# Another order of pairs in a quad's last slot, and the first norm's result turned in blocks on VectorE and placed by way of DRAM

## The chip, the cores and the metric

The kernel runs on one core of a Trainium2 chip (trn2). Its engines are TensorE (PE in the profile), VectorE (DVE), ScalarE (ACT), GpSimd (POOL) and SyncE (SP, which here only issues DMAs). The metric is the device time of one execution, in microseconds, on that core.

## The reference

One decoder layer over 16 sequences of 512 tokens with 256 features, all in float32. Attention has 16 heads of 16 features, a LoRA term on q and v, rotary positions and a causal mask. The feed-forward part is a product up to 1024, ten butterfly stages, Gelu, ten butterfly stages and a product down to 256. A layer norm without weights follows each part.

```python
q = query @ wq + query @ Aq @ Bq * 4.0
k = query @ wk
v = query @ wv + query @ Av @ Bv * 4.0
q, k = rope(split_heads(q)), rope(split_heads(k))
attn = softmax(where(causal, -1e9, q @ k.T / sqrt(16)))
x = layernorm(x + merge_heads(attn @ v) @ wo)          # the first norm
h = butterfly(x @ W_exp + b_exp, up_weights)
h = gelu(h + up_bias)                                  # exact
y = butterfly(h, down_weights) @ W_con + b_con + down_bias
x = layernorm(x + y)                                   # the second norm
```

Both butterflies are linear, so the kernel folds them into the two weight matrices once (`fold_tasks`), and then runs two plain products for each sequence.

## The kernel before

**Batches, quads, slots.** A sequence is called a batch, b from 0 to 15. Its 16 heads are handled as four quads of four heads, (c, par) with c and par in 0 and 1. The four heads of a quad lie in four groups of 32 rows of TensorE, and heads 0 and 1 are its pair 0, heads 2 and 3 its pair 1. The 512 x 512 scores of a head are cut in four blocks of 128 rows or columns, of widths 512, 384, 256 and 128 because of the causal mask. A quad takes five slots (`PER_QUAD = 5`), so that a batch takes 20 (`per`). The main loop runs over slots, `for s in range(-head, last)`. In this text u is a slot's place in its quad (s mod 5), and n its place among the 20 of a batch (s mod 20).

**Two passes over the scores.** Each slot holds two pieces of work. `largest` (L420 on TensorE, L429 on VectorE) computes scores of the quad of this slot to find each row's largest value: VectorE reads the score tile with a reduction into `junk` and `mx`. `weights` (L477, L494, L498) computes scores of the quad of 15 slots earlier (`behind`), transposed and with the largest already subtracted by an extra row. ScalarE takes their Exp from the score tile into `pT`, and POOL's affine_select clears the masked part. One slot later `weigh` (L521) multiplies pT with the values into `po`; after a quad's last group, `normalize_heads` copies po on ScalarE (L540) and issues two or three DMAs on SP.

**Score tiles.** There are only two, of two PSUM banks each: `pb` (pair0 in the code) and `pa` (pair1). In slots with u from 0 to 3, `weights` writes pb, read by ScalarE, and `largest` writes pa, read by VectorE. The two work on different pairs of heads, so that their matmuls run side by side in different row groups. In slots with u = 4 both write half of each of the two tiles, pair 0 in pb and pair 1 in pa.

**Order.** The schedule is written by hand. Every engine works through its instructions in program order, and the program's order is: the matmuls of a slot, then what reads them, then `weigh` of earlier slots, then the list `others[s]` (filled by `add(s, f, ...)`), then the list `holes[s]`, then fold tasks. The matmuls outside the scores thus stand between the scores of one slot and the next, while ScalarE and VectorE empty pb and pa; they are called fillers below. With s = 20 b, the fillers and the other steps that matter stand at:

- `project_v` (L383, one matmul pair for each of four blocks t), four slots; its result is copied into `vaug` on ScalarE (L390)
- `start_projection` (L337, 16 matmuls of 128x512), for the next batch, four at s + 10, as holes; followed by `turn` (rotary, on POOL) and `part`
- `project_out` (L559) at s + 41 and s + 42; then the first norm: `spread` (VectorE, then a pow on POOL), `offset` (VectorE), `centre` (ScalarE, four instructions)
- `turn_x1` (L616, L617) at s + 45: eight transposes on TensorE with `ident`, two copies on VectorE into `x1T`, then one addition of biases on POOL (L621)
- `hidden` (L633): eight chunks hc, two a slot, from s + 46; copied to `h` by ScalarE or VectorE
- `gelus` (L651): eight instructions on ScalarE, at s + 50, with a table load before and after
- `contract` (L660): four blocks t in two halves, at s + 51, 52, 53, 55, 56, 58, 60, 63; after a second half VectorE adds (L668) and takes the statistics
- `spread`, `offset`, `centre`, `store` for the second norm at s + 63 to s + 68

So the later steps of batch b run two batches after its scores began, beside the scores of batches b + 1 and b + 2. The last two batches have an order of their own behind the last score slots (`edge`, `end`).

Of the kernel before, what the change touches and what calls it, by code (L numbers as in the profile page):

```python
# [11 lines left out]
F32 = mybir.dt.float32  # L12
# [5 lines left out]
P = 128  # L18
# [15 lines left out]
def decoder_layer(  # L34
# [345 lines left out]
    def project_v(b, t):  # L380
        pv = bank(f"pvv_{b}_{t}", [P, D])
        for d in range(NC):
            nc.tensor.matmul(  # L383
                pv,
                xTs[b][:, d, t * P : (t + 1) * P],
                wv_sb[:, d, :],
                start=(d == 0),
                stop=(d == NC - 1),
            )
        nc.scalar.copy(  # L390
            vaugs[b % 2][:, t, :, 1 : 1 + 2 * HG].rearrange("p g (h i e) -> p g h i e", h=2, e=2)[
                :, :, :, :, 0
            ],
            pv.rearrange("p (g h i) -> p g h i", h=2, i=DH),
        )
# [14 lines left out]
    def largest(b, c, par, placed):  # L410

        q, k_ = qz[b % NR][c], kz[b % NR][c]
        mms, later = [], []
        for block, pair, ps, at in placed:
            n, t = width(block), NT - 1 - block
            for i in range(2):
                g = 2 * pair + i
                rows = slice(HG * g, HG * g + (HG if par else DH))
                mms.append(
                    lambda i=i, rows=rows, at=at, n=n, t=t, ps=ps: nc.tensor.matmul(  # L420
                        ps[:, i, at : at + n],
                        q[rows, par, t * P : n],
                        k_[rows, par, 0:n],
                        start=True,
                        stop=True,
                    )
                )
                later.append(
                    lambda i=i, at=at, n=n, t=t, g=g, ps=ps: nc.vector.tensor_tensor_reduce(  # L429
                        out=junk[:, 0:n],  # L430
                        in0=ps[:, i, at : at + n],
                        in1=causal[:, T - n : T],
                        scale=-1.0,
                        scalar=HUGE,
                        op0=ALU.add,
                        op1=ALU.min,
                        accum_out=mxs[c][:, par, g, t : t + 1],
                    )
                )
        return mms, lambda: [f() for f in later]  # L440

    def place_largest(b, c):

# [16 lines left out]
    def weights(b, c, par, placed):  # L460

        qt, kt = qz[b % NR][c], kz[b % NR][c]
        group = placed[0][0]
        key = ("pT", b, c, par, group)
        if key not in state:
            state[key] = ppool.tile(
                [P, NG, T], F32, tag="pT", name=f"pT_{b}_{c}_{par}_{group}"
            )
        pT = state[key]
        mms = []  # L470
        for block, pair, ps, at in placed:
            n = width(block)
            for i in range(2):
                g = 2 * pair + i
                rows = slice(HG * g, HG * g + (HG if par else DH + 1))
                mms.append(
                    lambda i=i, rows=rows, at=at, n=n, k=block, ps=ps: nc.tensor.matmul(  # L477
                        ps[:, i, at : at + n],
                        kt[rows, par, k * P : (k + 1) * P],
                        qt[rows, par, k * P : T],  # L480
                        start=True,
                        stop=True,
                    )
                )

        def after():
            for pair in range(2):
                mine = [(block, ps, at) for block, r, ps, at in placed if r == pair]
                if not mine:
                    continue  # L490
                n = sum(width(block) for block, _, _ in mine)
                ps, at = mine[0][1:]
                heads = slice(2 * pair, 2 * pair + 2)
                nc.scalar.activation(pT[:, heads, 0:n], ps[:, :, at : at + n], AF.Exp)  # L494
                at = 0
                for block, _, _ in mine:
                    diag = pT[:, heads, at : at + P]
                    nc.gpsimd.affine_select(  # L498
                        out=diag,
                        in_=diag,  # L500
                        pattern=[[0, 2], [1, P]],
                        compare_op=ALU.is_ge,
                        fill=0.0,
                        base=0,
                        channel_multiplier=-1,
                    )
                    at += width(block)

        return mms, after

    def weigh(b, c, par, group):
        pT = state.pop(("pT", b, c, par, group))
# [95 lines left out]
            )  # L608


    def turn_x1(b, c):
        if c == 0:
            state["x1T", b] = ring2.tile([P, NC, T], F32, tag="x1T", name=f"x1T_{b}", bufs=1)
        pt = bank(f"pt1_{b}_{c}", [P, NT, P])
        for t in range(NT):
            nc.tensor.transpose(pt[:, t, :], zs[b][:, t, c * P : (c + 1) * P], ident)  # L616
        nc.vector.tensor_copy(  # L617
            state["x1T", b][:, c, :], pt.rearrange("p t q -> p (t q)")
        )
        if c == NC - 1:  # L620
            nc.gpsimd.tensor_tensor(  # L621
                zs[b],
                zs[b],
                bias2[:, 0:1, :].to_broadcast([P, NT, D]),
                ALU.add,
            )

    def hidden(b, hc, fused=False):
        if hc == 0:
# [2 lines left out]
        for c in range(NC):  # L632
            nc.tensor.matmul(  # L633
                ph,
                wup[:, c, hc * P : (hc + 1) * P],
                state["x1T", b][:, c, :],
                start=(c == 0),
                stop=(c == NC - 1),
            )
# [72 lines left out]
    for b in range(B):  # L712
        s = b * per
        if b > 0:

            at = {1: (-16, -11, -13, -9), B - 1: (-1, 10, 10, 14)}.get(b, (-3, -1, 4, 14))
            for t in range(NT):
                add(s + at[t], project_v, b, t)
        if b + 1 < B:

            add(s - head * (b == 0), load_xT, b + 1)
            at = {0: (2, 5, 7, 10), 1: (3, 6, 8, 11)}.get(b, (10, 10, 10, 10))
            for i, (c, side) in enumerate(chains):
                holes.setdefault(s + at[i], []).append(
                    lambda b=b, side=side, c=c: start_projection(b + 1, side, c)
# [2 lines left out]
                for step in range(3):  # L728
                    add(turning + step, turn, b + 1, side, c, step)
                for step in range(1 + side):  # L730
                    add(turning + (6 if i == 3 else 4) + step, part, b + 1, side, c, step)
        add(s + 9, load_x, b)
        add(s + 11, place_largest, b, 0)
        add(s + 21, place_largest, b, 1)
        for c in range(NC if b + 1 < B else 1):
            for t in range(NT):
                at = (27, 28, 29, 31) if c == 0 else (36, 37, 39, 40)
                add(s + (at[t] if b + 1 < B else 29 + t), normalize, b, c, t)
        if b + 1 < B:
            for t in range(NT):  # L740
# [1 line left out]
            add(s + 42, spread, 1, b)  # L742
            add(s + 43, offset, 1, b)
            add(s + 44, centre, 1, b)
            for c in range(NC):
                add(s + 45 + (b + 2 == B), turn_x1, b, c)
        if b + 2 < B:
            for hc in range(NHC):
                add(s + 46 + hc // 2, hidden, b, hc)
            holes.setdefault(s + 50, []).insert(0, lambda b=b: gelus(b))  # L750
            for t in range(NT):
                for half in range(2):
                    at = (11, 12, 13, 15, 16, 18, 20, 23)[2 * t + half]
                    if b + 3 == B and t == NT - 1:
                        at = (23, 25)[half]
                    add(s + 40 + at, contract, b, t, half)
            add(s + 63 + 2 * (b + 3 == B), spread, 2, b)
            add(s + 66, offset, 2, b)
            add(s + 68, centre, 2, b)
            add(s + 68, store, b)  # L760

# [41 lines left out]
    first, second = fold_tasks()  # L803
    fold = first + second
    tasks_at = dict(zip(range(2, behind), (0, 1, 2, 3, 4, 4, 5, 5, 5, 6, 9, 11, 14)))
    for s in range(behind, 2 * per + 5):
        tasks_at[s] = len(first) + -(-len(second) * (s - behind + 1) // (2 * per + 5 - behind))
    ahead = 0
    given = 0
    due = deque()  # L810
# [12 lines left out]
    for s in range(-head, last):  # L823
# [4 lines left out]
            if 0 <= n < B * per  # L828
        ]
        parts = []  # L830
        step = 2
        if kinds and not (len(kinds) == 1 and kinds[0][2] % 2):
            u = kinds[0][2]
            pair0 = ps_b.tile([P, 2, T], F32, tag="b", name=f"pb_{s}")
# [147 lines left out]
```

## Time and profile before

| | us |
|---|---|
| median of 3 runs | 1386.91 |
| range of the runs | 1386.61 to 1389.14 |
| profiled execution | 1387.34 |
| its span, first to last instruction | 1385.6 |
| TensorE busy | 1355.0 (98%) |
| VectorE busy | 916.0 (66%) |
| ScalarE busy | 713.1 (51%) |
| POOL busy | 509.5 (37%) |
| mean granted TensorE clock | 0.987 |

Reading the rows: an instruction row gives its start in the span and its duration in microseconds, the engine, the line, the operation, what it writes <- what it reads, and its shapes; square brackets at its end give the idle time of the engine before it and who ended that. Matmuls are pipelined and their ends modelled, so a row of TensorE ends some 0.07 us after the next can start. A float32 matmul is two instructions. Rows of the chain of waits give start, duration and the work that the end of the span hung on. A window row gives each engine's busy time in a stretch, then the granted clock and the DMA share.

### The profile page before, as it was taken

To read this page: it belongs to the slowest core of one execution; us is meant where nothing else is said; L and a number is where in the kernel's file an instruction comes from. 1 tells how busy PE (TensorE), PEld (TensorE's weight loads), DVE (VectorE), ACT (ScalarE), POOL (GpSimd) and SP (SyncE) were. 2 spreads that over 40 slices of the span, in tenths; PEclk is the share of its full clock that TensorE was granted. 3 is DMA by queue.
4 is the path that set the end of the run, shared out by engine and by line. 5 is a ranking of instruction groups with operands and counts; after the bars stand their busy time and mean duration, and the time that the engine had idled before them with its cause. 6 is when DMAs were issued, how large, how long until landed. Compare 5 with 4: busy or idle time off the path is not lost.

```text
span 1385.6 us, 23937 instructions
## 1 busy us (share of the span) xinstructions
PE 1355.0 (98%) x8760; PEld 719.7 (52%) x8760; DVE 916.0 (66%) x2937; ACT 713.1 (51%) x1101; POOL 509.5 (37%) x777
## 2 busy tenths in 40 slices
PE   8999999999999999999999999999999999998998
PEld 4445545455454545545454555545455554544455
DVE  5667757667585766758576675857677585765532
ACT  2576454554545455454545555454555545454543
POOL 3425215344352534435153433515343351531311
PEclk9899999999999999999999999999999999999999
DMA  5311010110201011020101102010110201010000
GB/s 169 117 40 48 25 55 29 42 42 29 74 29 66 29 43 41 29 74 29 66 29 43 40 29 72 31 66 29 43 40 29 74 29 67 14 43 9 29 12 31
DMA packets 45685, 63.49 MB, mean 46 GB/s; under 512 B 5752, under 2 KB 26232, under 8 KB 45568
## 3 DMA queue, kind: packets, MB, share of 16 engines
q1 hardware_dynamic: 41680, 56.42, 11.5%
q10 hardware_dynamic: 3888, 5.55, 1.3%
q8 instruction: 69, 1.13, 0.3%
q14 instruction: 48, 0.39, 0.1%
HBM read 23.40 MB, written 8.91 MB: 23 GB/s over the span
## 4 chain that ended last, share of the span: by engine, by line
PE 94%; DVE 3%; ACT 2%; issue 1%; DMA 0%; POOL 0%; POOLq 0%; DVEq 0%; ACTq 0%
PE pb L477 20%; PE py L660 17%; PE ph L633 17%; PE po L521 11%; PE pqk L337 8%; PE pa L420 5%; PE pvv L383 5%; PE pwo L559 4%; PE pd L267 2%; PE pb L420 1%; DVE junk L429 1%; PE pa L477 1%; PE pt L616 1%; ACT pT L494 1%; PE fold L219 1%
## 5 line engine op out<-in xcount | busy, mean ns | idle before, releaser
L429 DVE CUSTOM_DVE_ANT_0 junk<-pa,causal 128x384 bf16<-128x384 f32 (+2 forms) x878 | 438.5, 499 | 216.0 <-PE pa L420 182.8
L494 ACT ACTIVATE pT<-pb 128x1024 f32<-128x1024 f32 (+1 forms) x314 | 293.9, 936 | 372.1 <-PE pa L420 255.6
L498 POOL TENSOR_SCALAR_AFFINE_SELECT pT<-pT 128x256 f32<-128x256 f32 x512 | 201.9, 408 | 755.2 <-ACT pT L494 751.1
L477 PE MATMUL pb<-qz,kz 17*128 17x512 f32 (+2 forms) x1756 | 330.2, 475 | 11.6 <-ACT pT L494 9.9
L420 PE MATMUL pa<-kz,qz 32*128 32x384 f32 (+3 forms) x1756 | 323.8, 468 | 1.7 <-DVE mx L429 1.7
L660 PE MATMUL py<-wdn,h 128*128 128x256 f32 x1024 | 254.1, 392 | 1.4 <-ACT h L651 1.4
L633 PE MATMUL ph<-x1T,yb 128*128 128x512 f32 x512 | 237.6, 608 | 1.8 <-DVE x1T L617 1.8
L477 PEld LDWEIGHTS pb<-qz,kz 17*128 17x128 f32 (+1 forms) x1756 | 142.5, 184 | 173.5 <-issue 92.3
L660 PEld LDWEIGHTS py<-wdn,h 128*128 128x128 f32 x1024 | 185.8, 190 | 75.8 <-issue 37.0
L521 PE MATMUL po<-pT,vaug 128*32 128x512 f32 (+3 forms) x2048 | 180.1, 447 | 0.0
L420 PEld LDWEIGHTS pa<-kz,qz 32*128 32x128 f32 (+1 forms) x1756 | 149.3, 185 | 22.4 <-ACT vaug L390 9.6
L633 PEld LDWEIGHTS ph<-x1T,yb 128*128 128x128 f32 x512 | 92.9, 191 | 125.4 <-issue 98.6
L553 DVE RECIPROCAL sums<-sums 128x128 f32<-128x128 f32 x128 | 121.2, 947 | 0.0
L646 ACT COPY h<-ph 128x512 f32<-128x512 f32 x86 | 50.3, 585 | 134.8 <-PE ph L633 134.8
L337 PE MATMUL pqk<-xT,wqk 128*128 128x512 f32 x256 | 119.1, 616 | 0.0
L429 DVE CUSTOM_DVE_ANT_0 junk<-pb,causal 128x256 bf16<-128x256 f32 (+3 forms) x146 | 63.6, 435 | 73.5 <-ACT pT L494 66.1
L521 PEld LDWEIGHTS po<-pT,vaug 128*32 128x32 f32 x2048 | 47.1, 109 | 101.7 <-issue 88.9
L429 DVE DVE_READ_ACCUMULATOR2_ANT mx<- 128x1 f32 x1024 | 84.6, 83 | 0.0
L337 PEld LDWEIGHTS pqk<-xT,wqk 128*128 128x128 f32 x256 | 48.1, 194 | 61.1 <-issue 57.6
L602 ACT ACTIVATE z<-z,norm 128x256 f32<-128x256 f32 x128 | 66.8, 593 | 24.9 <-DVE norm L595 24.8
L365 POOL TENSOR_TENSOR swap<-swap,rope_sb 128x512 f32<-128x512 f32 x62 | 78.7, 1270 | 0.0
L668 DVE TENSOR_TENSOR z<-py,z 128x256 f32<-128x256 f32 x64 | 27.1, 424 | 77.0 <-PE py L660 75.3
(88 smaller groups left out, 1342.9 us busy)
## 6 DMA issues: line engine op xcount, KB each, us to landing
xT<-in_xT SPq DMA_DIRECT2D x16, 512.0 KB
swap<-qz SPq DMA_DIRECT2D x64, 128.0 KB
swap<-kz SPq DMA_DIRECT2D x64, 128.0 KB
z<-in_x SPq DMA_DIRECT2D x16, 512.0 KB
sums<-x SPq DMA_DIRECT2D x64, 128.0 KB
out_y<-z SPq DMA_DIRECT2D x15, 512.0 KB
x<-x SPq DMA_DIRECT2D x32, 128.0 KB
early<-in_wexpT ACTq DMA_DIRECT2D x1, 1028.0 KB
```

The lines of the kernel that those rows point to most:

```text
L337: nc.tensor.matmul(pq, wqk[:, d, e : e + P], xTs[b][:, d, :], start=(d == 0), stop=(d == NC - 1))
L365: engine.tensor_tensor(swap, swap, rope_sb[:, 1, :], ALU.mult)
L383: nc.tensor.matmul(pv, xTs[b][:, d, t * P : (t + 1) * P], wv_sb[:, d, :], start=(d == 0), stop=(d == NC - 1),)
L420: lambda i=i, rows=rows, at=at, n=n, t=t, ps=ps: nc.tensor.matmul(ps[:, i, at : at + n], q[rows, par, t * P : n], k_[rows, par, 0:n], star ...
L429: lambda i=i, at=at, n=n, t=t, g=g, ps=ps: nc.vector.tensor_tensor_reduce(out=junk[:, 0:n], in0=ps[:, i, at : at + n], in1=causal[:, T - n ...
L477: lambda i=i, rows=rows, at=at, n=n, k=block, ps=ps: nc.tensor.matmul(ps[:, i, at : at + n], kt[rows, par, k * P : (k + 1) * P], qt[rows, ...
L494: nc.scalar.activation(pT[:, heads, 0:n], ps[:, :, at : at + n], AF.Exp)
L498: nc.gpsimd.affine_select(out=diag, in_=diag, pattern=[[0, 2], [1, P]], compare_op=ALU.is_ge, fill=0.0, base=0, channel_multiplier=-1,)
L521: nc.tensor.matmul(po[HG * g : HG * (g + 1), k * P : T], vaugs[b % 2][:, k, NG * c + g, first : first + HG], pT[:, g, at : at + n], start= ...
L553: nc.vector.reciprocal(sums[:, ts], sums[:, ts])
L633: nc.tensor.matmul(ph, wup[:, c, hc * P : (hc + 1) * P], state["x1T", b][:, c, :], start=(c == 0), stop=(c == NC - 1),)
L660: nc.tensor.matmul(py, state["h", b][:, hc, t * P : (t + 1) * P], wdn[:, hc, :], start=(hc == 0), stop=(hc == NHC - 1),)
```

## The change

It has four parts.

- In slots with u = 4, `largest` takes pair 1 (pa) first, where `weights` takes pair 0 (pb) first. Matmuls are issued two by two in place of four by four, and the readers alternate: Exp of one pair, reductions of the other, Exp of the other, reductions of the first.
- For batches 0 to 13, `turn_x1_by_blocks` takes the place of `turn_x1`. VectorE transposes the first norm's result in blocks of 32 x 32 (four instructions), SP writes them to a DRAM tile with four DMAs, and reads `x1T` back with a fifth. The matmuls of `hidden` read x1T through an access pattern with runs of 32 elements. The addition of biases is a step of its own, two slots later.
- Steps move: `hidden` two slots later, `gelus` and the next batch's projections from u = 0 to u = 2, `contract`, the second norm, `store`, `load_x` and part of `normalize` later.
- For the last batch, `project_v` moves as a whole to slot 12, with its copies on VectorE.

The diff, cut to its core:

```diff
@@ -387,7 +387,8 @@
                 start=(d == 0),
                 stop=(d == NC - 1),
             )
-        nc.scalar.copy(
+        copy = nc.vector.tensor_copy if b + 1 == B else nc.scalar.copy
+        copy(
             vaugs[b % 2][:, t, :, 1 : 1 + 2 * HG].rearrange("p g (h i e) -> p g h i e", h=2, e=2)[
                 :, :, :, :, 0
             ],
@@ -437,7 +438,8 @@
                         accum_out=mxs[c][:, par, g, t : t + 1],
                     )
                 )
-        return mms, lambda: [f() for f in later]
+        pairs = [later[i : i + 2] for i in range(0, len(later), 2)]
+        return mms, [lambda both=both: [f() for f in both] for both in pairs]
 
     def place_largest(b, c):
 
@@ -483,30 +485,28 @@
                     )
                 )
 
-        def after():
-            for pair in range(2):
...
+        def after(pair):
+            mine = [(block, ps, at) for block, r, ps, at in placed if r == pair]
+            n = sum(width(block) for block, _, _ in mine)
+            ps, at = mine[0][1:]
+            heads = slice(2 * pair, 2 * pair + 2)
+            nc.scalar.activation(pT[:, heads, 0:n], ps[:, :, at : at + n], AF.Exp)
...
+        pairs = sorted({pair for _, pair, _, _ in placed})
+        return mms, [lambda pair=pair: after(pair) for pair in pairs]
 
     def weigh(b, c, par, group):
         pT = state.pop(("pT", b, c, par, group))
@@ -608,6 +608,14 @@
             )
 
 
+    def add_biases(b):
+        nc.gpsimd.tensor_tensor(
+            zs[b],
+            zs[b],
+            bias2[:, 0:1, :].to_broadcast([P, NT, D]),
+            ALU.add,
+        )
+
     def turn_x1(b, c):
         if c == 0:
             state["x1T", b] = ring2.tile([P, NC, T], F32, tag="x1T", name=f"x1T_{b}", bufs=1)
@@ -618,12 +626,23 @@
             state["x1T", b][:, c, :], pt.rearrange("p t q -> p (t q)")
         )
         if c == NC - 1:
-            nc.gpsimd.tensor_tensor(
-                zs[b],
-                zs[b],
-                bias2[:, 0:1, :].to_broadcast([P, NT, D]),
-                ALU.add,
-            )
+            add_biases(b)
+
+    def turn_x1_by_blocks(b):
+
+
+        blocks = ring2.tile([P, D // HG, NT, HG], F32, tag="blocks", name=f"blocks_{b}", bufs=1)
+        for t in range(NT):
+            nc.vector.transpose(blocks[:, :, t, :], zs[b][:, t, :])
+        turned = dram.tile([D // HG, HG, NG, P], F32, tag="turned", name=f"turned_{b}")
+        for n in range(NG):
+            nc.sync.dma_start(
+                turned[:, :, n, :].rearrange("f j k -> j f k"),
+                blocks[HG * n : HG * (n + 1)].rearrange("j f t i -> j f (t i)"),
+            )
+        x1T = ring2.tile([P, NC, T], F32, tag="x1T", name=f"x1T_{b}", bufs=1)
+        nc.sync.dma_start(x1T, turned.rearrange("(c f) j n k -> (f j) c (n k)", c=NC))
+        state["x1T", b] = x1T.rearrange("p c (n t i) -> p c t n i", t=NT, i=HG)
 
     def hidden(b, hc, fused=False):
         if hc == 0:
@@ -633,7 +652,7 @@
             nc.tensor.matmul(
                 ph,
                 wup[:, c, hc * P : (hc + 1) * P],
-                state["x1T", b][:, c, :],
+                state["x1T", b][:, c],
                 start=(c == 0),
                 stop=(c == NC - 1),
             )
@@ -713,13 +732,13 @@
         s = b * per
         if b > 0:
 
-            at = {1: (-16, -11, -13, -9), B - 1: (-1, 10, 10, 14)}.get(b, (-3, -1, 4, 14))
+            at = {1: (-16, -11, -13, -9), B - 1: (12, 12, 12, 12)}.get(b, (-3, -1, 4, 14))
             for t in range(NT):
                 add(s + at[t], project_v, b, t)
         if b + 1 < B:
 
             add(s - head * (b == 0), load_xT, b + 1)
-            at = {0: (2, 5, 7, 10), 1: (3, 6, 8, 11)}.get(b, (10, 10, 10, 10))
+            at = {0: (2, 5, 7, 10), 1: (3, 6, 8, 11)}.get(b, (12, 12, 12, 12))
             for i, (c, side) in enumerate(chains):
                 holes.setdefault(s + at[i], []).append(
                     lambda b=b, side=side, c=c: start_projection(b + 1, side, c)
@@ -728,13 +747,13 @@
                 for step in range(3):
                     add(turning + step, turn, b + 1, side, c, step)
                 for step in range(1 + side):
-                    add(turning + (6 if i == 3 else 4) + step, part, b + 1, side, c, step)
-        add(s + 9, load_x, b)
+                    add(turning + (6 if i > 1 else 4) + step, part, b + 1, side, c, step)
+        add(s + 20, load_x, b)
         add(s + 11, place_largest, b, 0)
         add(s + 21, place_largest, b, 1)
         for c in range(NC if b + 1 < B else 1):
             for t in range(NT):
-                at = (27, 28, 29, 31) if c == 0 else (36, 37, 39, 40)
+                at = (29, 30, 31, 33) if c == 0 else (36, 37, 39, 40)
                 add(s + (at[t] if b + 1 < B else 29 + t), normalize, b, c, t)
         if b + 1 < B:
             for t in range(NT):
@@ -742,22 +761,25 @@
             add(s + 42, spread, 1, b)
             add(s + 43, offset, 1, b)
             add(s + 44, centre, 1, b)
+        if b + 2 == B:
             for c in range(NC):
-                add(s + 45 + (b + 2 == B), turn_x1, b, c)
+                add(s + 46, turn_x1, b, c)
         if b + 2 < B:
+            others[s + 45].insert(0, lambda b=b: turn_x1_by_blocks(b))
+            add(s + 47, add_biases, b)
             for hc in range(NHC):
-                add(s + 46 + hc // 2, hidden, b, hc)
-            holes.setdefault(s + 50, []).insert(0, lambda b=b: gelus(b))
+                add(s + 48 + hc // 2, hidden, b, hc)
+            holes.setdefault(s + 52, []).insert(0, lambda b=b: gelus(b))
+            at = (13, 15, 16, 18, 20, 23, 25, 26)
+            if b + 3 == B:
+                at = (13, 15, 16, 18, 20, 23, 24, 25)
             for t in range(NT):
                 for half in range(2):
-                    at = (11, 12, 13, 15, 16, 18, 20, 23)[2 * t + half]
-                    if b + 3 == B and t == NT - 1:
-                        at = (23, 25)[half]
-                    add(s + 40 + at, contract, b, t, half)
-            add(s + 63 + 2 * (b + 3 == B), spread, 2, b)
-            add(s + 66, offset, 2, b)
-            add(s + 68, centre, 2, b)
-            add(s + 68, store, b)
+                    add(s + 40 + at[2 * t + half], contract, b, t, half)
+            add(s + 40 + at[-1], spread, 2, b)
+            add(s + 68, offset, 2, b)
+            add(s + 69, centre, 2, b)
+            add(s + 70, store, b)
 
 
 
@@ -803,8 +825,8 @@
     first, second = fold_tasks()
     fold = first + second
     tasks_at = dict(zip(range(2, behind), (0, 1, 2, 3, 4, 4, 5, 5, 5, 6, 9, 11, 14)))
-    for s in range(behind, 2 * per + 5):
-        tasks_at[s] = len(first) + -(-len(second) * (s - behind + 1) // (2 * per + 5 - behind))
+    for s in range(behind, 2 * per + 7):
+        tasks_at[s] = len(first) + -(-len(second) * (s - behind + 1) // (2 * per + 7 - behind))
     ahead = 0
     given = 0
     due = deque()
@@ -828,7 +850,6 @@
             if 0 <= n < B * per
         ]
         parts = []
-        step = 2
         if kinds and not (len(kinds) == 1 and kinds[0][2] % 2):
             u = kinds[0][2]
             pair0 = ps_b.tile([P, 2, T], F32, tag="b", name=f"pb_{s}")
@@ -838,23 +859,26 @@
                 for r, ps in enumerate((pair0, pair1)):
                     parts.append(fn(*quad, place([(k, r) for k in GROUPS[u // 2]], ps)))
             elif u == PER_QUAD - 1:
-                step = 4
+
+
+                blocks = [(2, r, ps) for r, ps in enumerate((pair0, pair1))]
                 for i, (fn, quad, _) in enumerate(kinds):
-                    parts.append(
-                        fn(*quad, [(2, r, ps, i * 2 * P) for r, ps in enumerate((pair0, pair1))])
-                    )
+                    parts.append(fn(*quad, [(*block, i * 2 * P) for block in blocks]))
+                    blocks.reverse()
             else:
                 for i, (fn, quad, _) in enumerate(kinds):
                     blocks = [(k, (r + i) % 2) for k, r in SLOTS[u]]
                     parts.append(fn(*quad, place(blocks, (pair0, pair1)[i])))
             if kinds[0][0] is weights and (u % 2 if len(kinds) == 2 and u < 4 else True):
                 due.append((s, (*kinds[0][1], u // 2)))
-        for i in range(0, max([len(p[0]) for p in parts], default=0), step):
+        for i in range(0, max([len(p[0]) for p in parts], default=0), 2):
             for p in parts:
-                for f in p[0][i : i + step]:
+                for f in p[0][i : i + 2]:
                     f()
-        for p in parts:
-            p[1]()
+        for i in range(max([len(p[1]) for p in parts], default=0)):
+            for p in parts:
+                for f in p[1][i : i + 1]:
+                    f()
         while due and due[0][0] < (s if m < B * per else s - 1):
             weigh(*due.popleft()[1])
         for f in others[s]:
```

More of the change, by code (lines that the diff above doesn't have):

```diff
@@ L484, in weights @@
                 )
-        def after():
-            for pair in range(2):
[L488 to L505, printed above, removed]
-                    )
-                    at += width(block)
-        return mms, after
+        def after(pair):
[4 more added lines that the diff above has]
+            nc.scalar.activation(pT[:, heads, 0:n], ps[:, :, at : at + n], AF.Exp)
+            at = 0
+            for block, _, _ in mine:
+                diag = pT[:, heads, at : at + P]
+                nc.gpsimd.affine_select(
+                    out=diag,
+                    in_=diag,
+                    pattern=[[0, 2], [1, P]],
+                    compare_op=ALU.is_ge,
+                    fill=0.0,
+                    base=0,
+                    channel_multiplier=-1,
+                )
+                at += width(block)
+        pairs = sorted({pair for _, pair, _, _ in placed})
+        return mms, [lambda pair=pair: after(pair) for pair in pairs]
     def weigh(b, c, par, group):
```

## The prediction, made before the result was known

> **What bounds the kernel now.** I read the page first: which engine is full, and which the chain of waits runs through.
>
> ```profile
> PE 1355.0 (98%) x8760; PEld 719.7 (52%) x8760; DVE 916.0 (66%) x2937; ACT 713.1 (51%) x1101; POOL 509.5 (37%) x777
> PE 94%; DVE 3%; ACT 2%; issue 1%; DMA 0%; POOL 0%; POOLq 0%; DVEq 0%; ACTq 0%
> ```
>
> TensorE bounds it. But "busy" hides something, so next I read the timeline of TensorE over one batch. A batch takes 80.68 us (its 16 pqk matmuls start at 678.46 and 759.14), 20 slots of the loop over s; n below is a slot's place among the 20, u = n mod 5. Slot 14 (u = 4) ends with po and pvv, slot 15 (u = 0) begins with pb:
>
> ```profile
> 696.75 1.07 PE L521 MATMUL po<-pT,vaug 128*32 128x384 f32 x16
> 697.75 1.13 PE L383 MATMUL pvv<-wv_sb,xT 128*128 128x256 f32 x4
> 698.81 1.13 PE L477 MATMUL pb<-qz,kz 17*128 17x512 f32 x4
> 699.52 1.13 PE L420 MATMUL pa<-kz,qz 32*128 32x512 f32 x4
> ...
> 703.07 0.70 PE L477 MATMUL pb<-qz,kz 17*128 17x512 f32 x2
> 703.08 0.70 PE L420 MATMUL pa<-kz,qz 32*128 32x512 f32 x2
> ```
>
> In slot 16 pb and pa start together and the scores take 1.06 us. In slot 15 pa starts 0.71 us late: the scores take 1.77. The same view has 0.69 in slot 0, 0.51 in slot 5: 1.91 us a batch that no row calls idle, since pb's matmuls run alone meanwhile. Why is pa late? The timelines of ScalarE and VectorE in slot 14:
>
> ```profile
> 696.80 0.60 ACT L494 ACTIVATE pT<-pb 128x512 f32<-128x512 f32 x1 [2.04 <-PE pb L420]
> 697.29 0.59 ACT L494 ACTIVATE pT<-pa 128x512 f32<-128x512 f32 x1
> ```
> ```profile
> 697.43 0.42 DVE L429 CUSTOM_DVE_ANT_0 junk<-pb,causal 128x256 bf16<-128x256 f32 x1 [1.80 <-ACT pT L494]
> 698.47 0.42 DVE L429 CUSTOM_DVE_ANT_0 junk<-pa,causal 128x256 bf16<-128x256 f32 x1
> 698.94 0.43 DVE L429 CUSTOM_DVE_ANT_0 junk<-pa,causal 128x256 bf16<-128x256 f32 x1
> ```
>
> Only at u = 4 do both readers use both tiles. VectorE wants pb first, and waits for the Exp on pb to end (697.40); it reaches pa at 698.47, ends at 699.37, and pa's matmuls go 0.15 later.
>
> Then the chain of waits, for the transposes and two stalls near the end:
>
> ```profile
> 735.65 1.02 PE pt L616 x8
> ...
> 1247.48 4.38 ACT h L651 x7
> ...
> 1301.87 2.31 DVE norm L595
> ```
>
> **Part 1, transposes.** Eight matmuls of 1.02 us in the chain leave slot 5, for 14 of 16 batches: **-14.3 us**. The x1T copies (1.28 us of VectorE) go too.
>
> **Part 2, order of pairs.** Same matmuls. With E the end of a u = 4 slot's scores: Exp on pb E+0.1 to 0.7, VectorE on pa at once, E+0.1 to 1.05 (a pair took 0.90 above), Exp on pa 1.1 to 1.7, VectorE on pb 1.15 to 2.05, free for TensorE at E+2.2. Matmuls cover 2.06 us (po 1.00, pvv 1.06). So slots 0, 5 and 15 start 0.17 late each, not 0.71, 0.69, 0.51: 1.4 us a batch. That pattern stands in 13 batches: **-18.2 us**. Bounds: 0 if the wait only moves to ScalarE, 1.9 if nothing is late. Behind the later Exp on pa stand centre and the pvv copy: slot 5's Exp starts near S+1.9 (S the start of slot 5) instead of S+1.2, covered since slot 6 starts at S+3.55. Its affine_select moves 0.5 later on POOL; po reads that result a slot on.
>
> **Part 3, x1T by way of DRAM.** On VectorE at slot 5: reductions until S+2.7, then four transposes of 128x256. No such row; nearest are BATCH_NORM_STATS2 on 128x256 from SBUF (428 ns) and the adds of 128x256 (424). I take 0.43, bounds 0.3 and 0.86: done at S+4.4. They must clear before slot 6's reductions (S+4.7), and at 0.43 do. On SP: the two x copies' DMAs come first (ScalarE's x copy ends about S+3.5, two issues of 0.5 to 0.6), so SP is free at S+4.6; four writes at 0.55 an issue, the last at S+6.2. The timeline of SP gives the rest:
>
> ```profile
> 719.10 0.54 SPq L90 DMA_DIRECT2D xT<-in_xT  x1
> 723.38 0.33 SPq L450 DMA_DIRECT2D rows<-mT  x1
> 724.79 1.17 SPq L455 DMA_DIRECT2D qz<-rows  x2
> ```
>
> rows, 16 KB in pieces of 512 B to DRAM, is waited for 1.41 us after its issue; a 128 KB sums copy, issued at 718.54, has moved its last byte by 720.3 in the DMA view. So 1.8 us for the last write, and the read is issued at S+8.05. xT is the same read (512 KB, rows of 2 KB): issue 719.10, last bytes by 722.4: 3.3 us. **x1T lands at S+11.35**, bounds 10.4 (smaller transfers, 0.3 transposes) and 14. Queued behind on SP meanwhile: nothing until kz<-ones_row in slot 9.
>
> A rule speaks against this part. The Trainium skill, "VectorE: DVE Perf Modes", section "The three transpose paths", warns that a plain DMA that transposes by strides is 19 times slower than the crossbar's 1309 ns for a 128x128 tile. By it, sixteen such tiles would arrive some 400 us late; by the rows above, 11 us in all. I go by the rows, since the pieces here are 512 B and 2 KB, as in rows and xT: the element-wise part is done on VectorE.
>
> **Part 4, the emptied slot.** hidden moves to slots 8 to 11, contract to 13, 15, 16, 18, 0, 3, 5, 6, projections and Gelus to 12. Fillers stay at 1.9 us or more except slot 7, left with po alone, 1.0 us. Before has such a slot late in batch 14:
>
> ```profile
> 1191.21 1.07 PE L521 MATMUL po<-pT,vaug 128*32 128x512 f32 x8
> 1192.45 0.91 PE L477 MATMUL pb<-qz,kz 17*128 17x384 f32 x4 [0.17 <-ACT pT L494]
> 1193.26 0.59 PE L420 MATMUL pa<-kz,qz 32*128 32x384 f32 x2
> ```
>
> That cost 1.05 us (pa at 1193.26, not 1192.21). In slot 7 VectorE also comes 0.2 late: py of slot 6 ends at S+6.55, then add, stats and spread (0.42 + 0.43 + 0.18 + 0.2, with gaps) until S+7.95, where the scores would let it start at S+7.8. So 1.25 in slot 8: scores end at S+10.92, then hidden waits for x1T, 0.43 more. Against no wait (S+9.67) that is 1.68 us, **+23 us** over 14 batches. Bounds 1.05 (x1T early, VectorE free) and 4.4 (x1T at S+14).
>
> Costed at nothing: add_biases on POOL (2.35 us, moved to slot 7; POOL 37% busy, contract's add comes at slot 15), load_x and store (long before use), Gelus at slot 12: Exp to 2.2, table 1.28, Gelus 5.0, table 1.28 make 9.8, and slot 13's scores end at 10.2, covered by pqk's 7.06; without it up to 1.7 a batch. hidden reading x1T in runs of 32: no row, taken as equal; a 10% slowdown would be 1.45 us a batch.
>
> **Part 5, the end.** In batch 15 the Gelus keep TensorE waiting: slots 311 and 312 run from 1245.04 to 1261.43, 16.4 us where 7.3 is work. With the four pvv and po (5.24 us) over the Gelus, pT's next Exp ends at 10.8 where slot 14 could begin at 9.3: 1.5, and maybe a half-clock window, so -6.6. offset(2) now stands behind turn_x1, so x1T is not kept by POOL's norm: ph at about 1303.0, not 1304.83, and the half clock after it goes: -3.6. Four more u = 4 slots (299, 304, 314, 319) gain about 0.6: -2.5. **-12.7 us**, bounds -5 and -17.
>
> **Sum**: -14.3 - 18.2 + 23.5 - 12.7 = -21.7. The profiled execution took 1387.34 us (span 1385.6 and 1.7 around it), 0.4 above the median of 1386.91; from the median, 1365.2, said as 1365.
>
> **The rivals.** *x1T comes late enough to drop the clock.* TensorE's granted clock in the window table just after an idle gap of 1.84 us (1303.0 to 1304.83):
>
> ```profile
> 1304.00:1311.00 7.00, 6.17 (x20) 2.47 (x24) 4.08 (x7) 2.79 (x7) 1.59 (x5) 0.76 0.22 77
> ```
>
> 0.76 over 7 us is 3.4 us at half: 1.7 us lost. The Trainium skill, "TensorE: Matmul & The Clock Gate", section "Why this matters for your kernels", warns only of gaps over about 3 us. By it, x1T at S+12.4 costs just its 1.0 us more, 14 us in all, and the change still gains (1379); by the row, idle of 1.4 us after slot 8's stall may halve the clock, another 1.7. I go by the row: 14 x 2.7 = 38, **1403**. It decides from about S+12.2. For: two DRAM trips in series, transposes unmeasured, 1 us of margin. Against: each leg has a near row. Chance 0.18.
>
> *Order of pairs gives nothing*: the wait turns from VectorE to ScalarE and pb comes as late as pa did: +18, **1383**. For: pb is needed first. Against: the two readers then work at once. 0.10.
>
> *x1T early*: only slot 8's 1.05: **1356**. For: small transfers. Against: SP's queue of six. 0.19.
>
> The sum itself: 0.53.
>
> **How the numbers follow.** 1365 is the first case's. Its own spread (part 2 by 5, part 4 by 7, part 5 by 4, together about 10) joins the second and third rival: 1352 to 1385, leaving out the clock's case and little else. A measurement here tells 0.2%, 2.8 us, from no change. Faster 0.78 (0.53 + 0.19 and half of the second rival), same 0.04, slower 0.18.
>
> **What would show it.** Right: pb and pa together in slots 0, 5 and 15 within 0.2 us; VectorE on pa and Exp on pb at one time at u = 4; x1T's DMA landing some 11.3 us after slot 5 begins, and a wait for it of under 1 us ahead of ph; clock 1.0 through slots 8 to 10; batches of about 79.9 us. Wrong: ph waiting for the DMA over 1.4 us with the clock at half behind it; transposes over 0.8 us; ph matmuls slower; slot 8's stall absent.

## The result, and the profile after

| | before | changed |
|---|---|---|
| median, us | 1386.76 (4 runs) | 1407.20 (4 runs, 1404.51 to 1412.04) |
| profiled execution, us | 1387.34 | 1412.04 |
| its span, us | 1385.6 | 1410.3 |
| mean granted clock | 0.987 | 0.970 |

The ratio is 1.0151, with a 95% interval of 1.0114 to 1.0187: the change made the kernel slower by 1.5%, where 1.6% faster was forecast.

The page of the changed kernel, the lines that answer to those shown of before, and the group of the `hidden` matmuls:

```profile
PE 1354.3 (96%) x8648; PEld 712.0 (50%) x8648; DVE 912.9 (65%) x2969; ACT 710.5 (50%) x1097; POOL 509.9 (36%) x777
...
PE 81%; DMA 6%; ACT 4%; DVE 4%; SPq 2%; issue 2%; POOLq 0%; POOL 0%; DVEq 0%; ACTq 0%
PE ph L652 18%; PE pb L479 17%; PE py L679 13%; PE po L521 9%; PE pqk L337 8%; PE pwo L559 4%; PE pvv L383 3%; DMA x1T<-turned 3%; PE pa L421 3%; DVE junk L430 3%; DMA turned<-blocks 2%; PE pd L267 2%; PE pb L421 2%; ACT pT L493 1%; SPq L639 1%
...
L652 PE MATMUL ph<-x1T,yb 128*128 128x512 f32 x512 | 255.5, 646 | 17.1 <-DMA x1T<-turned 17.1
```

112 matmul instructions are gone and TensorE is busy as long as before: its clock was lower. In the chain of waits DMA had 0% and now has 6%, on the way to and from `turned`. The mean ph matmul grew from 608 to 646 ns.

Next, the stretch where that happens, slots 7 to 9 of one batch (slot 5 began at 341.11). The timeline of TensorE:

```profile
348.89 1.06 PE L521 MATMUL po<-pT,vaug 128*32 128x512 f32 x8
350.15 0.92 PE L479 MATMUL pb<-qz,kz 17*128 17x384 f32 x4 [0.20 <-ACT pT L493]
351.01 0.59 PE L421 MATMUL pa<-kz,qz 32*128 32x384 f32 x2
...
353.23 5.40 PE L652 MATMUL ph<-x1T,yb 128*128 128x512 f32 x8 [1.08 <-DMA x1T<-turned]
358.56 0.48 PE L479 MATMUL pb<-qz,kz 17*128 17x256 f32 x2
```

Three things stand in it: slot 8's pa comes 0.86 us after its pb; ph then waits 1.08 us for the DMA; and eight ph matmuls take 5.40 us, where eight took 3.70 before. The clock column of the window table says why:

```profile
352.40:356.00 3.60, 2.77 (x4) 1.18 (x5) 1.60 (x9) 0.63 (x1) 1.69 (x3) 0.71 0.07 27
```

0.71 over 3.6 us is half clock from 353.89 on: the trace has the clock at 0.50 for 3.41 us there. What is ph waiting for? The chain of waits through the same stretch (start, duration, what):

```profile
345.48 0.53 SPq L639
...
346.61 0.46 SPq L639
...
347.11 2.49 DMA turned<-blocks
...
349.74 3.44 DMA x1T<-turned
...
353.23 5.40 PE ph L652 x8
```

Four writes are issued one by one, the last is 2.49 us on its way, the read another 3.44. The transposes themselves are quick and early:

```profile
343.78 1.42 DVE L636 STREAM_TRANSPOSE blocks<-z 128x256 f32<-128x256 f32 x4
```

The other half of the change does what it should. Timelines of ScalarE and VectorE in slot 4, and of TensorE into slot 5:

```profile
339.18 0.60 ACT L493 ACTIVATE pT<-pb 128x512 f32<-128x512 f32 x1 [2.42 <-POOL pT L497]
340.00 0.60 ACT L493 ACTIVATE pT<-pa 128x512 f32<-128x512 f32 x1 [0.22 <-DVE mx L430]
```
```profile
339.06 0.42 DVE L430 CUSTOM_DVE_ANT_0 junk<-pa,causal 128x256 bf16<-128x256 f32 x1 [0.18 <-PE pa L479]
340.11 0.42 DVE L430 CUSTOM_DVE_ANT_0 junk<-pb,causal 128x256 bf16<-128x256 f32 x1
```
```profile
339.95 1.13 PE L383 MATMUL pvv<-wv_sb,xT 128*128 128x256 f32 x4
341.11 0.70 PE L479 MATMUL pb<-qz,kz 17*128 17x512 f32 x2
341.26 0.70 PE L421 MATMUL pa<-kz,qz 32*128 32x512 f32 x2
```

Exp on pb and the reductions of pa run at one time, then they change places; the next slot's pb is 0.10 late, its pa 0.15 after it.

To say where 24.7 us of span went, I read off the timeline of TensorE where slots 60, 300 and 320 begin, with pb's first matmul. For slots 60 and 300, before and then changed:

```profile
231.05 1.13 PE L477 MATMUL pb<-qz,kz 32*128 32x512 f32 x4
1199.54 1.13 PE L477 MATMUL pb<-qz,kz 32*128 32x512 f32 x4
```
```profile
238.96 0.70 PE L479 MATMUL pb<-qz,kz 32*128 32x512 f32 x2
1229.47 0.70 PE L479 MATMUL pb<-qz,kz 32*128 32x512 f32 x2 [1.10 <-ACT pT L493]
```

The batches between are called steady. This table is used for every experiment below.

| us | start to slot 60 | slots 60 to 300 | a batch of these 12 | 300 to 320 | 320 to end |
|---|---|---|---|---|---|
| before | 231.1 | 968.5 | 80.71 | 84.4 | 101.7 |
| changed | 239.0 | 990.5 | 82.54 | 79.8 | 101.1 |

So +7.9 early, +22.0 in the steady batches, -5.2 at the end. The moved `contract` steps take 3.9 us of matmuls out of the stretch before slot 60 and put them behind slot 320, so like for like it is about +11.8 early and -9 at the end.

### The profile page after: what moved, and what is told of

Same layout as the page of the kernel before. It is cut to its first block, busy times and chain, and to the rows that moved or that the text cites. A ratio compares the mean times of both kernels' runs of the same rounds, so it can differ in the third digit from the quotient of the medians.

```text
span 1410.3 us, 23814 instructions
## 1 busy us (share of the span) xinstructions
PE 1354.3 (96%) x8648; PEld 712.0 (50%) x8648; DVE 912.9 (65%) x2969; ACT 710.5 (50%) x1097; POOL 509.9 (36%) x777
## 3 DMA queue, kind: packets, MB, share of 16 engines
q8 instruction: 68, 1.11, 0.3%
## 4 chain that ended last, share of the span: by engine, by line
PE 81%; DMA 6%; ACT 4%; DVE 4%; SPq 2%; issue 2%; POOLq 0%; POOL 0%; DVEq 0%; ACTq 0%
PE ph L652 18%; PE pb L479 17%; PE py L679 13%; PE po L521 9%; PE pqk L337 8%; PE pwo L559 4%; PE pvv L383 3%; DMA x1T<-turned 3%; PE pa L421 3%; DVE junk L430 3%; DMA turned<-blocks 2%; PE pd L267 2%; PE pb L421 2%; ACT pT L493 1%; SPq L639 1%
## 5 line engine op out<-in xcount | busy, mean ns | idle before, releaser
L479 PE MATMUL pb<-qz,kz 17*128 17x512 f32 (+2 forms) x1756 | 335.0, 478 | 21.0 <-ACT pT L493 16.1
L421 PE MATMUL pa<-kz,qz 32*128 32x384 f32 (+3 forms) x1756 | 333.2, 479 | 3.3 <-DVE mx L430 3.3
L652 PE MATMUL ph<-x1T,yb 128*128 128x512 f32 x512 | 255.5, 646 | 17.1 <-DMA x1T<-turned 17.1
L652 PEld LDWEIGHTS ph<-x1T,yb 128*128 128x128 f32 x512 | 99.6, 204 | 146.5 <-issue 121.1
L421 PEld LDWEIGHTS pa<-kz,qz 32*128 32x128 f32 (+1 forms) x1756 | 145.3, 186 | 22.6 <-DVE mx L430 16.9
L430 DVE DVE_READ_ACCUMULATOR2_ANT mx<- 128x1 f32 x1024 | 84.4, 82 | 0.0
L365 POOL TENSOR_TENSOR swap<-swap,rope_sb 128x512 f32<-128x512 f32 x62 | 79.8, 1286 | 0.0
L383 PE MATMUL pvv<-wv_sb,xT 128*128 128x256 f32 x256 | 72.5, 410 | 0.0
```

The source lines that it names most:

```text
L365: engine.tensor_tensor(swap, swap, rope_sb[:, 1, :], ALU.mult)
L383: nc.tensor.matmul(pv, xTs[b][:, d, t * P : (t + 1) * P], wv_sb[:, d, :], start=(d == 0), stop=(d == NC - 1),)
L652: nc.tensor.matmul(ph, wup[:, c, hc * P : (hc + 1) * P], state["x1T", b][:, c], start=(c == 0), stop=(c == NC - 1),)
```

## The experiments

My theory after the result: the wait for x1T and the half clock behind it are the loss, and the order of pairs gained about what the sum gave it. Rivals: the moved steps and the empty slot 7, the DMA traffic or the strided reading of x1T, or the order of pairs itself. The first eight kernels below (e1 to e8) were timed on one chip, e9 to e11 on another.

**The order of pairs alone** (e1_pairs): the kernel before with the hunks of the diff on `largest`, `weights` and the end of the main loop, nothing else.

```diff
-                step = 4
+                blocks = [(2, r, ps) for r, ps in enumerate((pair0, pair1))]
...
+                    blocks.reverse()
```

> The kernel before with the other order of pairs alone. Theory (the order of pairs gains what the sum gave it, and the loss comes from the way through DRAM): pa late by 0.1 to 0.2 us in slots 0, 5 and 15 of a batch in place of 0.69, 0.51 and 0.71, batches of 79.2 us in place of 80.7, in all 1365 to 1370 us. Rival (the order of pairs itself costs something, early on or through the later Exp on pa): 1387 to 1395 us.

Measured: 1366.69 us, ratio 0.9851 (0.9831 to 0.9872). Batches of 79.60 us. TensorE's timeline out of slot 19:

```profile
705.55 1.13 PE L383 MATMUL pvv<-wv_sb,xT 128*128 128x256 f32 x4
706.72 0.70 PE L478 MATMUL pb<-qz,kz 32*128 32x512 f32 x2
706.84 0.70 PE L420 MATMUL pa<-kz,qz 16*128 16x512 f32 x2
```

pb could start at 706.61: 0.11 late, pa 0.12 after it, 0.23 in place of 0.69. The gain is 1.11 us a batch (1.4 in the sum). Part 2 stands; the rival of a costly or useless order falls.

**x1T turned on TensorE, in the changed schedule** (e2_turn).

```diff
-            others[s + 45].insert(0, lambda b=b: turn_x1_by_blocks(b))
-            add(s + 47, add_biases, b)
+            for c in range(NC):
+                add(s + 45, turn_x1, b, c)
```

> The changed kernel with x1T turned on TensorE again (eight transposes in slot 5, two copies on VectorE), every step else where the change put it. Theory (the wait for x1T and the half clock behind it cost 1.35 us and some 1.8 us a batch): no wait ahead of ph in slot 8, clock at full speed between slots 5 and 12, slot 8 still about 1 us long for want of matmuls in slot 7, batches of about 80.0 us with the transposes' 1.0 in them, 1370 to 1376 us. Rival (the moved steps and the emptied slot 7 are what costs): it stays within 10 us of 1407 us.

Measured: 1382.01 us, ratio 0.9967 (0.9950 to 0.9983). No half clock between slots 60 and 300, batches of 80.51 us. The wait's share of the theory holds: 25 us came back with 112 matmuls more. The total misses the 1370 to 1376 us that I expected. Slots 7 and 8 take 7.90 us where their matmuls fill 6.77: the emptied slot 7 costs 1.13 a batch, more than the transposes that stay. The moved steps are thus a loss of their own, 15 us against the order of pairs alone.

**Only the wait taken away** (e3_nowait).

```diff
+        tag = "x1T" if b else "x1T0"
...
-        state["x1T", b] = x1T.rearrange("p c (n t i) -> p c t n i", t=NT, i=HG)
+        x1T = x1T.rearrange("p c (n t i) -> p c t n i", t=NT, i=HG)
+        state["x1T", b] = state.setdefault("first x1T", x1T)
```

What this kernel leaves out is the dependence on the batch's own x1T: from batch 1 on `hidden` reads batch 0's, so that its result is another.

> The changed kernel, all its transposes and DMAs left in, but the hidden products of batches 1 to 13 read the x1T of batch 0, which landed long before (so its result is another): only the wait for x1T is gone. Theory: as in the changed kernel but 1.35 us less of waiting and hardly any half clock in a batch, batches of about 79 us, 1358 to 1366 us. Rival (the transfers themselves, or reading x1T in runs of 32 elements, slow other work): batches over 81 us, 1385 us or more.

Measured: 1375.64 us, ratio 0.9907 (0.9881 to 0.9934). The steady batches, 79.64 us, are what the theory asked for; the total is not, since slot 60 begins at 236.7. The window table behind slot 8, and the group of ph:

```profile
352.00:362.00 10.00, 10.00 (x41) 3.66 (x41) 5.29 (x14) 5.19 (x9) 0.81 (x2) 1.00 0.20 67
```
```profile
L654 PE MATMUL ph<-x1T,yb 128*128 128x512 f32 x512 | 238.0, 609 | 0.0
```

All the DMAs are there, and ph, reading in runs of 32, takes 609 ns as it took 608 from a plain x1T: the strides cost nothing, and of the transfers no cost to the steady batches shows. The wait with its half clock is 82.54 - 79.64 = 2.90 us a batch. Against e2_turn, the eight transposes are worth 0.87.

**TensorE kept busy while it waits** (e5_busy): two products without use ahead of `hidden` (the body of `busy_work` is left out here).

```diff
+            add(s + 48, busy_work, b)
             for hc in range(NHC):
```

> The changed kernel with two more 128x256 products (1.06 us of TensorE, their result unused) ahead of hidden in slot 8, so that TensorE is busy while it waits for x1T. Theory (the half clock behind the wait is a cost of its own, set off by the idle time): x1T lands when it did, idle ahead of ph falls from 1.35 to 0.3 us, the half clock after slot 8 goes, 15 to 20 us less: 1387 to 1392 us. Rival (the wait alone costs, the clock's share comes from elsewhere, as early on): no less than 1403 us; and if the products come on top, up to 1420 us.

Measured: 1391.87 us, ratio 1.0035 (1.0022 to 1.0049). TensorE's timeline in slot 8:

```profile
352.69 1.13 PE L650 MATMUL busy<-wv_sb,xT 128*128 128x256 f32 x4
354.02 3.70 PE L663 MATMUL ph<-x1T,yb 128*128 128x512 f32 x8 [0.20 <-DMA x1T<-turned]
```

15 us less for doing more. The half clock is gone from all 12 steady batches, and they take 81.08 us: the clock was 1.46 us a batch, the wait 81.08 - 79.64 = 1.44. The clock records agree: in the changed kernel's steady batches half clock lost 18.8 us, 1.56 a batch. The theory's finer claim, that the clock is a cost of its own, is shown.

**A projection in slot 7** (e4_pqk7), which fills the empty slot and brings TensorE to `hidden` later.

```diff
-            at = {0: (2, 5, 7, 10), 1: (3, 6, 8, 11)}.get(b, (12, 12, 12, 12))
+            at = {0: (2, 5, 7, 10), 1: (3, 6, 8, 11)}.get(b, (7, 12, 12, 12))
```

> The changed kernel with one of the four projections (1.77 us of TensorE) moved from slot 12 to the emptied slot 7. Theory (what costs is that TensorE reaches hidden before x1T lands): slot 8's late pa goes, TensorE reaches hidden 0.7 us later, the wait falls from 1.45 to about 0.7 us and the clock is no longer halved; slot 13's Exp comes some 0.5 us late behind the Gelus; batches of about 79.7 us, 1368 to 1376 us. Rival (the Gelus, with 1.77 us less over them, become the wait, or the trip through DRAM gets later too): batches over 81 us, 1388 us or more.

Measured: 1386.14 us, ratio 1.0003 (0.9985 to 1.0021). Between theory and rival. Slot 8's late pa is gone, and only one half-clock stretch is left in the steady batches. But batches take 80.69 us: the wait is still 0.8 in the mean, and the Gelus, with fewer matmuls over them, now stop slot 14. From TensorE's timeline:

```profile
342.45 3.70 PE L652 MATMUL ph<-x1T,yb 128*128 128x512 f32 x8 [0.32 <-DMA x1T<-turned]
...
363.94 5.42 PE L337 MATMUL pqk<-xT,wqk 128*128 128x512 f32 x12
...
373.46 0.48 PE L479 MATMUL pb<-qz,kz 32*128 32x256 f32 x2 [1.10 <-ACT pT L493]
```

**The early steps undone** (e6_early), on e2_turn: fold tasks over `2 * per + 5`, `load_x` at s + 11, `part` with `i == 3`.

> The kernel with x1T turned on TensorE in the changed schedule, with three of the moved steps undone: fold tasks end at slot 45 and not 47, load_x at s + 11 and not s + 20, part of the third chain two slots earlier. Theory (the moved steps cost the first three batches, which in the changed kernel lost 8 us by slot 60 with 3.9 us of contract less in them): slot 60 begins 5 to 8 us sooner, 1374 to 1377 us in place of 1382. Rival (the loss early on is where the half-clock windows happen to fall): within 3 us of 1382 us.

Measured: 1376.36 us, ratio 0.9922 (0.9903 to 0.9941), 5.7 less than e2_turn; slot 60 at 228.2, not 233.3. As the theory said, but see the next two.

**Both** (e8_both): e4_pqk7 with the same three steps undone.

> The changed kernel with a projection in slot 7 and the three moved steps of the early slots undone. Theory: the two gains add, 1361 to 1368 us, about as fast as the order of pairs alone. Rival (the early loss is chance): as the kernel with the projection in slot 7 alone, within 3 us.

Measured: 1383.52 us, ratio 0.9978 (0.9964 to 0.9992), 2.6 less than e4_pqk7 (slot 60 at 227.4, not 231.8). That is what the rival said (within 3 us); the theory missed the total, as it did for its base.

**The changed kernel again** (e9_again).

> The changed kernel once more, for a second profile. Theory (what the first three batches lose depends on where the half-clock windows fall, and is no fixed price of the moved steps): slot 60 begins 3 us or more away from the 238.96 us of the first profile, batches again about 82.5 us. Rival (a fixed price): slot 60 within 2 us of 238.96.

Measured: 1406.07 us, one run. Batches of 82.58 us again, but slot 60 at 233.0, not 239.0. In the first profile 37.5 us ahead of slot 60 ran at half clock, in this one 17.1. So 6 us of the early loss are no fixed price, and the stretches at half clock differ with them. What the three early steps cost for good, between 0 and 5.7 us, stays open: two pairs of kernels say 5.7 and 2.6, and one kernel varies by as much.

**Two edits for the end on top of the order of pairs** (e7_tail): `project_v` of the last batch all in slot 10 with its copies on VectorE, and the second norm's `offset` of batch 13 two slots later.

```diff
-            at = {1: (-16, -11, -13, -9), B - 1: (-1, 10, 10, 14)}.get(b, (-3, -1, 4, 14))
+            at = {1: (-16, -11, -13, -9), B - 1: (10, 10, 10, 10)}.get(b, (-3, -1, 4, 14))
...
-            add(s + 66, offset, 2, b)
+            add(s + 66 + 2 * (b + 3 == B), offset, 2, b)
```

> The kernel before with the order of pairs and two edits for the end: the last batch's project_v all in slot 10 with its copies on VectorE, and the second norm's offset of batch 13 behind the turning of batch 14. Theory (the sum's part for the end): slots 300 to 320 shorten by about 3 us and slots 325 to 330 by about 3.5, from 1366.7 to 1358 to 1361 us. Rival (the stalls only move, to slots 299 and 314, which lose their filler): 1364 us or more.

Measured: 1364.65 us, ratio 0.9834 (0.9817 to 0.9851). From slot 300 to the end 175.3 us against e1_pairs' 181.2, near the 6.5 expected; the total, 2.0 below e1_pairs, lies in the rival's range, since slot 60 begins at 233.6 against 228.8 with the same steps up to there. I ran both again, on one chip, five rounds.

> The kernel before with the order of pairs alone, again, beside the next one on the same chip. Theory: 1366 to 1367 us, batches of 79.6 us, slot 60 at 228 to 234 us (228.8 in the first profile).

> The order of pairs with the two edits for the end, again. Theory (the end gains some 6 us by itself, of which the first profile lost 5 early on by the clock's windows): slots 300 to the end 175.3 us as before, slot 60 nearer to 229 than to 233.6 in part of the runs, median 1360 to 1365 us, below the order of pairs alone. Rival (the two edits gain nothing that lasts): the same time within 1.5 us.

Measured: e10_pairs 1366.22 us (0.9858, 0.9833 to 0.9882), e11_tail 1363.17 us (0.9833, 0.9806 to 0.9860); slot 60 at 227.0 and 230.1. The edits for the end are worth 2 to 3 us in the median, and the order of pairs with them is the fastest kernel of the study, 1.7% under the kernel before and some 3% under the changed one.

## Why the prediction was wrong

By its own parts, per steady batch:

| part | forecast | measured | from |
|---|---|---|---|
| transposes off TensorE | -1.02 | -0.87 | e3_nowait against e2_turn |
| order of pairs | -1.40 | -1.11 | e1_pairs against before |
| emptied slot 7 | +1.25 | +1.13 | slots 7 and 8 of e2_turn |
| wait for x1T | +0.43 | +1.44 | e5_busy against e3_nowait |
| clock after it | 0 | +1.46 | changed against e5_busy |
| sum | -0.74 | +2.05 | changed against before: +1.83 |

The rows come from different kernels and overlap by 0.2. The first three held in the main; the order of pairs fell short mostly in slot 5, where slots 4 and 5 together became 0.19 us shorter, not 0.34.

**The step that failed is the landing of x1T: "So 1.8 us for the last write" and "last bytes by 722.4: 3.3 us".** In the 13 batches after the first, the last write took 2.62 us from its issue to the issue of the read (2.50 to 2.83), and the read 3.59 to ph (3.26 to 3.77): together 1.1 longer than forecast. Sum for the batch shown: the last write issued 6.0 us after slot 5 began (forecast 6.2), x1T there at 12.1, not 11.35; the mean of the 13 batches is 12.3.

Why? I had followed both near rows to their last byte in the DMA view, but what waits goes on later. The window table shows it for the batch above: the four writes' bytes, the time from the last of them to the issue of the read, the read up to its last byte, and the time from there to ph. The last two columns are the DMA share and GB/s.

```profile
346.50:349.25 2.75, 2.75 (x27) 1.75 (x29) 2.18 (x9) 0.69 (x2) 0.41 (x1) 1.00 0.81 191
349.25:349.74 0.49, 0.49 (x8) 0.00 (x0) 0.46 (x3) 0.49 (x1) 0.43 (x1) 1.00 0.00 0
349.74:352.83 3.09, 2.21 (x20) 0.99 (x16) 1.75 (x9) 1.18 (x2) 3.09 (x4) 1.00 0.59 170
352.83:353.23 0.40, 0.00 (x1) 0.00 (x1) 0.40 (x1) 0.20 (x1) 0.40 (x1) 1.00 0.00 0
```

Over the 13 batches these two times without a byte are 0.48 and 0.41 us in the mean, so 0.9 of the 1.1. The profile before had such a time too: the rows copy moved its last byte at 724.41, and SP issued what waited for it at 724.79. To the last byte alone, the read took 3.19 us, 0.1 less than forecast, and the last write 2.14, 0.34 more. For those 0.34 the near row, a copy of 128 KB within SBUF in 64 pieces of 2 KB, was not near enough: the four writes go to DRAM in 1024 pieces of 512 B and are on their way together. Which of these differences it was, no run here separates. The Trainium skill, "DMA: Bandwidth & Descriptors", section "Anatomy of one DMA", gives 2.0 us and the bytes at 436 GB/s for a DMA of GpSimd's path; by it an estimate of 2.3 and 3.2 us for these two, which SP issues: nearer for the write, short for the read.

**The second failure follows from the first: the clock, put at nothing in the sum.** I gave its case 0.18, "from about S+12.2". x1T landed past that edge in 9 of the 13 batches, and 8 of these 9 lost clock, as did 1 of the other 4. Idle ahead of ph was 1.15 to 2.17 us in those that lost clock (0.07 more than the row's bracket, for the modelled end), and 0.67, 0.79, 1.10 and 1.42 in the four that did not. The price of 1.7 us was right for seven of the nine (5.40 against 3.70); in the other two the half clock lasted 6.8 us in place of 3.4. The rival's 1403 us was near the 1407 measured. Weighing row against page, I was right to go by the row: the skill's "TensorE: Matmul & The Clock Gate", section "Why this matters for your kernels", warns of gaps over about 3 us, and 1.15 us sufficed here.

**The end** gained about 9 us like for like, forecast 12.7. **Early** I forecast nothing; the first profile lost 11.8 like for like, the second 5.9. How much of that lasts is open, as above.

Right: no cost for the strided reading (609 against 608 ns), none on POOL; the transposes at 0.355 us each lay within the bounds of 0.3 and 0.86. Right too was to go against the rule on transposes by strides in Part 3, since x1T landed at 12.3 us; but its some 400 us count sixteen tiles where x1T is eight of 128x128, so the estimate by that page is some 200. Gelus at slot 12 cost nothing in the changed kernel; "without it up to 1.7 a batch" was borne out by e4_pqk7, where a cover thinner by 1.77 us cost 1.17.

Even with no wait at all the change gains nothing over the order of pairs: e3_nowait's batch is 79.64 us, e1_pairs' 79.60. What leaving out the transposes saves, the slot emptied for the DMA's sake takes back.

## What to carry to other kernels

A transfer that takes the place of matmuls on a full TensorE must land before TensorE gets there with a margin of a microsecond or more: here being late cost 2.9 us a batch, half of it the wait and half the clock after it. Cost each leg of a trip through DRAM from issue to the next issue, or the instruction, that waits for it, and not to its last byte: the difference was 0.4 to 0.5 us a leg. And where two engines read the same two score tiles, let them begin at different tiles: here that alone was 1.5%.

## What was not expected of the hardware

All stretches at half clock in the trace of the changed kernel begin on one grid: 268.56, 353.89 and 435.81 us lie 25 and 24 times 3.413 us apart, and so with the others; each of the other traces has such a grid. That may be why 1.15 us of idle lost the clock in one batch and 1.42 did not in another. No run moved a wait against the grid by intent, but e9_again, the same kernel, did so by chance. Slot 108's idle, 1.37 and 1.36 us in the two profiles, began at 0.64 of a step of the grid in the first and lost clock; in the second it began at 0.91 and lost none. Slot 308's, 0.67 and 0.65 us, began at 0.88 and lost none; at 0.79 it did. In the 26 batches of the two profiles (the first batch of each left out), idle that began in the first 0.85 of a step lost clock, and of the seven that began later only one of 2.91 us did. Where the idle falls thus decides beside its length. What stands ahead of it seems to count as well: in e4_pqk7, with a fuller slot 7, 1.53 us of idle that began at 0.64 lost nothing.

The 15360 packets of 512 B in the changed kernel, 14336 of them from the writes to `turned`, took 33 ns in the mean; the 1024 packets of that size in the kernel before took 28.
